# Who starts a tile's sum: ScalarE takes the first expert's weighted bias, with six sum buffers and another order of 20 expert tiles

## The chip, the cores and the metric

The kernel runs on one core of a Trainium2 chip. Its time is device microseconds (us) of one execution; a lower number is better. The core has engines that run side by side and each execute their own queue of instructions strictly in order: TensorE (PE, matrix products and transposes; its weight loads are listed apart as PEld), VectorE (DVE), ScalarE (ACT) and GpSimd (POOL). SyncE (SP) issues DMAs. An instruction that has to wait for another engine, or for a DMA to land, holds up everything that stands behind it in its own queue.

## What is computed

The input `x` is 16 rows of 512 tokens, 128 numbers each, in float32. With `xn` the layer-normalised `x`, the result is

```
x + attention(xn) + experts(xn)
```

Attention is linear with a decay: `scores = (q k^T) * decay^(distance)`, causal, then `scores @ v @ o_w`. The experts are a mixture of four small networks, of which each token uses two:

```
logits = xn @ router_w + router_b + load_balancer
rw, sel = top_k(logits, 2);  rw = softmax(rw)
e0 = (silu(xn @ w1) * (xn @ w3)) @ w2
e1 = gelu(linear chain of xn @ c1w + c1b) @ c2w + c2b
e2 = two layer norms and a relu network on xn, then @ gen_w + gen_b
e3 = gelu(xn @ ml_w1 + ml_b1) @ ml_w2 + ml_b2
out = sum over the two chosen experts of  rw * e
```

So a token's result begins with weight times bias: experts 1, 2 and 3 have an output bias (`c2b`, `gen_b`, `ml_b2`), expert 0 has none.

## The kernel before

**Sorting tokens by pair of experts.** There are six pairs of experts and six lists in DRAM (`LISTS`, L28). Each list is cut into tiles of two to four chunks of 128 tokens; there are 20 tiles and 66 chunks, which is a little room over the 64 chunks of tokens. The 16 rows are taken in five groups (2, 2, 4, 4, 4 rows). When a group is normalised and its router logits are there, VectorE finds each token's pair and its place in the list (`route`, `count`, `placed`), and POOL scatters the normalised rows to the lists with one indirect DMA for each chunk (`send`, 64 of them, L489). A tile may be loaded when the group that fills it has been sent; `TURN` (L38) gives the order of the 20 tiles and each one's group.

**One row.** `load_x` (L218) fetches it on SP; VectorE takes its moments (`stats`, L458 to L462), POOL the inverse square root (`inv`, L467), VectorE the offset (`offs`, L472), ScalarE writes the normalised row into the buffer that is later sent (`norm`, L477), PE transposes it (`turn`), ScalarE copies that out of PSUM (`turned`), PE multiplies by the q, k, v and router weights (`proj`), ScalarE copies q, k, v (`values`) and VectorE the logits (`logits`, L579). Rows x0 to x10 have buffers of their own and are fetched at once in the first microseconds; x11 to x15 wait for buffers.

**Attention** goes in four quads of four rows (`attention`, L762): `keys` (PE) needs the `values` of the quad's last row, then `score` (PE), `scored` (VectorE, four instructions), `near` (PE), `nsum` (VectorE), `outs` (PE), `total` (VectorE) and `store` (SP).

**One tile** (`Tile.steps`, L996), called @k by its place in `TURN`: load `L` (SP), transpose `T` (PE), copy `TT` (ScalarE); `B`, the weighted biases that start the sum `o`; for each of the two experts its hidden products (`ga`, `gb`, `H`, `U`, `F` on PE; the functions on ScalarE; the products on VectorE), its output products `Y` on PE and the joins `J` on VectorE (`o = y * weight + o`, L946); and for each chunk a scatter `X` on POOL that adds `o` to the output in DRAM (66 of them, L489). Expert 2 has two layer norms on the way. Each of them goes PE, VectorE (`Su`, `Sv`), POOL (`Iu`, `Iv`), VectorE (`Ou`, `Ov`), ScalarE (`Nu`, `Nv`), PE (`Zu`, `Zv`).

**The order of the work.** All these steps are handed to a small planner in the kernel (`emit`, L158). It knows a cost in us for each step, a rank, a number of buffers for each kind of tile (`ROOM`, L115) and the times from which inputs are there; for row b among the first eleven it takes 4.75 + 1.25 b us (L804). It simulates the engines, always takes the step that can start first (within 0.25 us the one of lowest rank), and calls its function; the instructions then stand in each engine's queue in that order. `AHEAD` (L46) shifts the ranks of rows, tiles, biases and quads. So a change of a cost, a rank or a buffer count moves instructions in every queue. Where PE would stand idle early on, the planner puts single matmuls of ones, `fill0` to `fill24` (L356), whose results nobody reads.

**The biases in before** (`biases`, L882) are all on VectorE: one `tensor_scalar` for each chunk (L891, 66 in all), and one `scalar_tensor_tensor` more for each chunk of a tile that has no expert 0 (L893, 38 in all). `o` has four buffers.

Of the kernel before, what the change touches and what calls it, by code (L numbers as in the profile page):

```python
# [10 lines left out]
AF = mybir.ActivationFunctionType  # L11
ALU = mybir.AluOpType
# [7 lines left out]
GROUPS = (2, 2, 4, 4, 4)  # L20
# [5 lines left out]


LISTS = [  # L28
    ((0, 1), (3, 4, 4, 4)), ((0, 2), (3, 2)), ((0, 3), (4, 4)),
    ((1, 2), (3, 3, 4, 3)), ((1, 3), (2, 4, 3, 4, 4, 3)), ((2, 3), (3, 2)),  # L30
]
NL = len(LISTS)
LR = 16 * 512
# [2 lines left out]


TURN = [  # L38
    ((1, 2), 0, 1), ((1, 3), 0, 0), ((0, 1), 0, 1), ((0, 2), 0, 3), ((0, 1), 1, 2), ((1, 2), 1, 2),
    ((1, 2), 2, 4), ((1, 2), 3, 4), ((0, 1), 2, 3), ((2, 3), 0, 3), ((1, 3), 1, 2), ((1, 3), 2, 2),  # L40
    ((0, 1), 3, 4), ((2, 3), 1, 4), ((0, 3), 0, 3), ((1, 3), 3, 3), ((0, 2), 1, 4), ((1, 3), 4, 4),
    ((0, 3), 1, 4), ((1, 3), 5, 4),
]
FILL = 25

AHEAD = {"rows": -2.0, "tiles": 62.0, "biases": -5.0, "quads": (9.0, -36.0, -27.0, -27.0)}  # L46
LAST = 3


# [39 lines left out]
def decay_attention__plus__routed_experts(  # L89
# [10 lines left out]
    nc = tc.nc  # L100
    B, T, D = x.shape
    NC = T // P
# [12 lines left out]
    ROOM = {  # L115
        "bank": 8, "pay1": 2, "pay2": 5, "x": 11, "xnT": 3, "qkv": 2, "kT": 1, "qT": 1, "vs": 1, "S": 1, "sc": 4, "far": 1, "rT": 1,
        "xg": 4, "xT": 3, "th": 2, "h0": 1, "h1": 1, "h3": 1, "f": 1, "uv": 2, "z": 2, "h2": 2,
        "h2T": 1, "z2T": 1, "o": 4,
    }

    LATE = {"x": 3.0, "o": 3.2, "pay1": 2.6, "pay2": 2.6}
# [29 lines left out]
    PE, V, A, G, S = "PVAGS"  # L151
# [100 lines left out]
    F, M, C, R = views(fold_sb, FOLD), views(main_sb, MAIN), views(cols_sb, COLS), views(rows_sb, ROWS)  # L252
# [507 lines left out]
    quads = []  # L760

    def attention(b, a):  # L762

        rank = 5.0 * (b + QUAD - 1) + AHEAD["quads"][b // QUAD]
        of = range(QUAD)
# [23 lines left out]
    for g, m in enumerate(GROUPS):  # L789
# [3 lines left out]
        for b in range(first, first + m):  # L793
            k = NC * (b - first)
            r = Row(b, work, lambda c, k=k, q=q: q.entry(k + c)[:, :D])
            lg = q.lg[:, :, k : k + NC]
            rank = 5.0 * b - AHEAD["rows"] - (120.0 if b < 2 else 0.0)
            ends = [f"store{b}"]
# [29 lines left out]
            if b % QUAD == QUAD - 1:  # L828
                attention(q0, quads[-1])
        rank = 5.0 * (first + m) - AHEAD["rows"] - 50.0  # L830
        n = NC * m
# [17 lines left out]
    BIAS = {1: "c2b", 2: "gen_b", 3: "ml_b2"}  # L849

    class Tile:
# [30 lines left out]
        def biases(s):  # L882

            s.o = s.get("o", s.n, D)
            es = [e for e in s.pair if e in BIAS]
            for i, e in enumerate(es):
                w, bias = s.weight(e), R[BIAS[e]]
                for c in range(s.n):
                    o = s.o[:, c, :]
                    if i == 0:  # L890
                        nc.vector.tensor_scalar(o, bias, w(c), None, ALU.mult)  # L891
                    else:
                        nc.vector.scalar_tensor_tensor(o, bias, w(c), o, ALU.mult, ALU.add)  # L893

        def gate(s, i):
            s.ga = {**getattr(s, "ga", {}), i: bank(f"a_ps_{s.name}_{i}")[:, : s.N]}
# [99 lines left out]
        def steps(s, k, g, ranks):  # L996

            s.k, n, u = k, s.n, 0.2155 * s.n
            copy = 0.025 + 0.1125 * n
            biased, both = copy + 0.09, 0.06 + 0.135 * n  # L1000
            name = lambda q: f"{q}@{k}"

            def step(q, eng, us, fn, after=(), takes=(), rank=0.0):
                add(name(q), eng, us, fn, [name(a) if isinstance(a, str) else a for a in after],
                    [(kind, [name(e) for e in ends]) for kind, ends in takes], ranks + rank)
# [3 lines left out]
            parts = [range(c, min(c + size, n)) for c in range(0, n, size)]  # L1009
            joins = [f"J{e}.{c[0]}" for e in s.pair for c in parts]  # L1010
# [5 lines left out]
            def result(e, m, after, rank=0.0):  # L1016

                for i, c in enumerate(parts):
                    step(f"Y{e}.{c[0]}", PE, m * u / n * len(c), lambda c=c: s.y(e, c), ["B", *after] if i == 0 else [f"Y{e}.{parts[i - 1][0]}"],
                         [("bank", [f"J{e}.{c[0]}"])], rank + ending * (2.0 * i - (e == s.pair[1])))  # L1020
                    step(f"J{e}.{c[0]}", V, 0.26 * len(c), lambda c=c: s.joined(e, c), [f"Y{e}.{c[0]}"], rank=-2.0)
            last = sum(GROUPS[: g + 1]) * NC
            step("L", S, 2.3, s.load, [(f"send{g}.{NC * GROUPS[g] - 1}", 0.0)], [("xg", ["T", "to", "B", *joins])], -50.0)
            users = [f"{q}{i}" for e in s.pair for q, m in {0: (("ga", 4), ("gb", 4)), 1: (("H1", 2),), 2: (("U", 1),), 3: (("H3", 4),)}[e] for i in range(m)]
            step("T", PE, n * 0.11, s.turn, [(name("L"), 4.0)], [("bank", ["TT"]), ("xT", users)], -8.0)
            step("TT", A, copy, s.turned, ["T"], rank=-8.0)
            step("to", V, 0.08, s.numbers, [(name("L"), 4.0)])
            step("B", V, n * (0.2 if 0 in s.pair else 0.46), s.biases, [(name("L"), 4.0)], [("o", [f"X{c}" for c in range(n)])], AHEAD["biases"])
            if 0 in s.pair:
                for i in range(4):  # L1030
                    step(f"ga{i}", PE, u, lambda i=i: s.gate(i), ["TT"] + [f"ga{i - 1}"][: i], [("bank", [f"m{i}"]), ("th", [f"h{i}"])] + ([("h0", [f"Y0.{end}"])] if i == 0 else []))
# [11 lines left out]
            if 2 in s.pair:  # L1043
                def normed(key, after, bank, ends, head):
                    step(f"S{key}", V, 0.6 + 0.35 * n, lambda: s.summed(key), after, rank=head)
                    step(f"I{key}", G, 0.4 + 0.2 * n, lambda: s.inv(key), [f"S{key}"], rank=head - 100.0)
                    step(f"O{key}", V, 0.08, lambda: s.offs(key), [f"I{key}"], rank=head - 100.0)
                    step(f"N{key}", A, 0.02 + 0.385 * n, lambda: s.norm(key), [f"O{key}"], [("z", ends)], head)

                step("U0", PE, u, s.syn, ["TT"], [("bank", ["Su"]), ("uv", ["Nu"])], -7.0)  # L1050
                normed("u", ["U0"], "U0", ["R", "Zu"], -7.0)
                step("R", V, 0.12 + 0.27 * n, s.residual, ["Nu"], [("h2", ["Sv"])], -7.0)
                step("Zu", PE, n * 0.11, lambda: s.zturn("u"), ["Nu"], [("bank", ["ZZu"]), ("h2T", ["F0", "F1"])], -6.5)
                step("ZZu", A, copy + 0.2, lambda: s.zturned("u"), ["Zu"], rank=-6.5)
                for i in range(2):
                    step(f"F{i}", PE, u, lambda i=i: s.hid("f", i, M["f1w"], lambda: s.h2T), ["ZZu"] + [f"F{i - 1}"][: i], [("bank", [f"AF{i}"])] + ([("f", ["F"])] if i == 0 else []), -6.0)
                    step(f"AF{i}", A, biased, lambda i=i: s.act("f", i, 2, AF.Relu, C["f1b"]), [f"F{i}"], rank=-6.0)
                step("F", PE, 2 * u, s.ff2, ["AF0", "AF1"], [("bank", ["Sv"]), ("uv", ["Nv"])], -6.0)
                normed("v", ["F", "R"], "F", ["Zv"], -5.5)
                step("Zv", PE, n * 0.11, lambda: s.zturn("v"), ["Nv"], [("bank", ["ZZv"]), ("z2T", [f"Y2.{end}"])], -5.0)  # L1060
                step("ZZv", A, copy + 0.2, lambda: s.zturned("v"), ["Zv"], rank=-5.0)
                result(2, 1, ["ZZv"], -4.0)
# [3 lines left out]
    tiles = {}  # L1066
# [5 lines left out]
    for k, (pair, i, g) in enumerate(TURN):  # L1072
        tiles[pair, i].steps(k, g, AHEAD["tiles"] + 12.0 * k)

# [5 lines left out]
    f = "p g l -> p (g l)"  # L1080
# [29 lines left out]
    with tc.For_i(0, trips, 1) as i:  # L1110
# [20 lines left out]
        s = Dense(0, 3, 0, NC, "row")  # L1131
# [9 lines left out]
        for e in BIAS:  # L1141
            for c in range(NC):
                o = s.o[:, c, :]
# [78 lines left out]
```

## Time and profile before

| what | us |
|---|---|
| median of six runs | 302.32 (301.92 to 302.73) |
| the profiled execution, its own time | 302.81 |
| its span, first to last instruction | 301.1 |
| PE busy | 286.5, 2218 matmul instructions |
| VectorE busy | 203.5, 827 instructions |
| ScalarE busy | 159.8, 347 instructions |
| POOL busy | 204.7, 238 instructions |
| last output product of the last tile ends, last scatter starts | 291.3, 293.7 |

The profiled execution is 1.7 us longer than its span (time around the first and last instruction), and 0.5 us longer than the median of the runs. In the profile a line such as `L489` is the line of the kernel that recorded the instruction; the lines L146 (matmul) and L484 (transpose) are helpers that all PE work goes through. A group's row gives the count, the busy time in us and the mean length of one in ns. An engine's instructions overlap a little, so their distance from start to start is shorter than the length that is listed.

### The profile page before, as it was taken

Reading aid. Unit: us, or ns where it says so; the run is one execution under the profiler, and the core shown is the slowest. Engines: PE = TensorE matmul, PEld = TensorE weight load, DVE = VectorE, ACT = ScalarE, POOL = GpSimd, SP = SyncE. Lnnn points to the kernel's source line nnn. Section 1 sums busy time; section 2 is a strip of 40 time slices with the busy share of each in tenths; the row PEclk is TensorE's granted clock in tenths of the full one; section 3 lists DMA queues with packets and bytes.
Section 4 is the critical chain, followed back from the end, with each engine's and each line's share of the span. In section 5 each row is a group of like instructions: output and inputs, shape, how many; then the busy total and the mean of one; then the engine's idle time right before and its main releaser. Section 6 shows DMA issues by size and latency. Waiting matters only on the chain.

```text
span 301.1 us, 6542 instructions
## 1 busy us (share of the span) xinstructions
PE 286.5 (95%) x2218; PEld 223.2 (74%) x2218; DVE 203.5 (68%) x827; ACT 159.8 (53%) x347; POOL 204.7 (68%) x238
## 2 busy tenths in 40 slices
PE   8999999899999999999999999999999999999970
PEld 7899777788775768766678888758847797765960
DVE  3898899899878397848897676449747146635330
ACT  2889896966971324844473765524443326507020
POOL 5648978778877768888877758886642457183472
PEclk9999999999999999999999999999999999999995
DMA  6994174916321251335533243553222224023032
GB/s 174 307 300 170 42 242 120 312 51 188 102 98 61 89 184 57 69 30 76 69 29 50 25 85 48 73 75 37 36 23 50 49 27 59 7 27 26 8 31 22
DMA packets 33236, 26.55 MB, mean 88 GB/s; under 512 B 3632, under 2 KB 30512, under 8 KB 33072
## 3 DMA queue, kind: packets, MB, share of 16 engines
q0 software_dynamic: 11552, 8.92, 20.0%
q1 hardware_dynamic: 21072, 16.44, 18.2%
q10 hardware_dynamic: 576, 0.74, 0.8%
q8 instruction: 19, 0.31, 0.4%
q14 instruction: 17, 0.14, 0.2%
HBM read 12.09 MB, written 14.12 MB: 87 GB/s over the span
## 4 chain that ended last, share of the span: by engine, by line
PE 74%; DVE 12%; DMA 5%; POOL 3%; issue 2%; ACT 1%; ACTq 0%; POOLq 0%; SPq 0%; DVEq 0%
PE y_ps L146 27%; PE h_ps L146 15%; PE b_ps L146 8%; PE a_ps L146 8%; PE f_ps L146 7%; DVE sc L642 2%; DMA fold_sb<-in_fold_dram 2%; PE xT_ps L484 2%; PE proj_ps L146 2%; PE u_ps L146 2%; DVE st_x L458 1%; DMA x<-in_x_dram 1%; DMA lists<-pay,idx 1%; POOL rstd_x L467 1%; POOL out_dram L489 1%
## 5 line engine op out<-in xcount | busy, mean ns | idle before, releaser
L489 POOL DMA_INDIRECT out_dram<-o,to x66 | 103.7, 1571 | 52.1 <-DVE o L946 38.6
L489 POOL DMA_INDIRECT lists<-pay,idx x64 | 63.7, 995 | 18.6 <-issue 5.6
L946 DVE SCALAR_TENSOR_TENSOR o<-y_ps,xg,o 128x128 f32<-128x128 f32 x132 | 38.3, 344 | 48.6 <-PE y_ps L146 48.2
L146 PEld LDWEIGHTS y_ps<-main_sb,h 128*128 128x128 f32 x456 | 53.9, 192 | 5.4 <-issue 3.8
L146 PE MATMUL y_ps<-main_sb,h 128*128 128x128 f32 x456 | 54.9, 275 | 0.3 <-ACT kT L630 0.3
L922 ACT ACTIVATE h<-h_ps,cols_sb 128x512 f32<-128x512 f32 (+2 forms) x40 | 24.3, 612 | 29.8 <-PE h_ps L146 29.1
L146 PE MATMUL h_ps<-xT,main_sb 128*128 128x512 f32 (+2 forms) x80 | 33.7, 520 | 1.0 <-DVE x L701 1.0
L922 ACT ACTIVATE h<-h_ps,b_e 128x512 f32<-128x512 f32 (+2 forms) x28 | 17.6, 628 | 24.9 <-PE h_ps L146 24.6
L905 ACT ACTIVATE th<-a_ps 128x512 f32<-128x512 f32 (+2 forms) x32 | 17.2, 543 | 23.3 <-PE a_ps L146 23.0
L146 PE MATMUL a_ps<-xT,w_sb 128*128 128x512 f32 (+2 forms) x64 | 29.2, 543 | 0.0
L908 DVE SCALAR_TENSOR_TENSOR th<-th,a_ps 128x512 f32<-128x512 f32 (+2 forms) x32 | 19.4, 616 | 13.3 <-ACT th L905 12.9
L477 ACT ACTIVATE pay<-x,off_x,rstd_x 128x128 f32<-128x128 f32 x64 | 26.3, 486 | 2.9 <-DVE off_x L472 2.3
L146 PEld LDWEIGHTS y_ps<-sw_w2h,h 128*128 128x128 f32 x224 | 26.0, 192 | 1.0 <-issue 0.4
L146 PE MATMUL y_ps<-sw_w2h,h 128*128 128x128 f32 x224 | 26.6, 275 | 0.0
L146 PE MATMUL b_ps<-xT,w_sb 128*128 128x512 f32 (+2 forms) x64 | 26.0, 541 | 0.3 <-ACT xT L873 0.3
L146 PE MATMUL h_ps<-xT,w_e 128*128 128x512 f32 (+2 forms) x56 | 25.1, 539 | 0.0
L467 POOL TENSOR_TENSOR rstd_x<-ve_x,neg_half 128x4 f32<-128x4 f32 x16 | 16.5, 1035 | 8.9 <-DVE ve_x L462 5.9
L146 PEld LDWEIGHTS h_ps<-xT,main_sb 128*128 128x128 f32 x80 | 13.9, 191 | 8.6 <-issue 4.5
L913 DVE TENSOR_TENSOR h<-th,b_ps 128x512 f32<-128x512 f32 (+2 forms) x32 | 19.4, 618 | 1.2
L146 PEld LDWEIGHTS b_ps<-xT,w_sb 128*128 128x128 f32 x64 | 11.7, 190 | 10.0 <-issue 6.5
L146 PEld LDWEIGHTS a_ps<-xT,w_sb 128*128 128x128 f32 x64 | 11.1, 190 | 7.8 <-issue 5.0
L458 DVE BATCH_NORM_STATS2 st_x<-x 128x6 f32<-128x128 f32 x64 | 13.8, 279 | 4.6 <-DMA x<-in_x_dram 4.5
(185 smaller groups left out, 490.7 us busy)
## 6 DMA issues: line engine op xcount, KB each, us to landing
x<-in_x_dram SPq DMA_DIRECT2D x16, 256.0 KB, 5.3
out_dram<-x SPq DMA_DIRECT2D x16, 256.0 KB, 2.8
xg<-lists SPq DMA_DIRECT2D x9, 288.0 KB, 2.9
xg<-lists SPq DMA_DIRECT2D x8, 216.0 KB, 2.5
main_sb<-in_main_dram SPq DMA_DIRECT2D x1, 1216.0 KB, 7.4
out_dram<-o,to POOLq DMA_INDIRECT x66, 3.3
lists<-pay,idx POOLq DMA_INDIRECT x64, 2.3
lists<-none SPq DMA_DIRECT2D x6, 144.0 KB, 5.3
```

Source lines behind the costliest of these rows:

```text
L146: nc.tensor.matmul(o, lhsT, rhs, start=start, stop=stop)
L458: nc.vector.bn_stats(st[:, c, :], v(c))
L467: nc.gpsimd.tensor_tensor(rstd, ve, neg_half[:, :n], ALU.pow)
L477: nc.scalar.activation(o(c), v(c), AF.Identity, bias=off[:, c : c + 1], scale=rstd[:, c : c + 1])
L484: nc.tensor.transpose(pt[:, ts(c, P)], z(c), ident)
L489: i = nc.gpsimd.indirect_dma_start(out=o, out_offset=bass.IndirectOffsetOnAxis(ap=index, axis=0), in_=src, in_offset=None, bounds_check=n ...
L642: nc.vector.tensor_tensor(s.sc[i], s.sbanks[i].rearrange("p (c t) -> p c t", c=NC), near.unsqueeze(1).to_broadcast([P, NC, P]), ALU.mult,)
L905: nc.scalar.activation(s.th[i], s.ga[i], AF.Tanh, scale=0.5)
L908: nc.vector.scalar_tensor_tensor(s.th[i], s.th[i], 1.0, s.ga[i], ALU.add, ALU.mult)
L913: nc.vector.tensor_tensor(s.h0[:, i, :], s.th[i], s.gb[i], ALU.mult)
L922: nc.scalar.activation(getattr(s, key)[:, i, :], s.hb[key, i], func, bias=bias[:, i : i + 1])
L946: nc.vector.scalar_tensor_tensor(o, s.py[e, chunks[0]][:, c, :], w(c), o, ALU.mult, ALU.add)
```

## The change

The first weighted bias of a tile is written by ScalarE, as an activation `Copy` with the weight as its scale (66 instructions); the second, for the 38 chunks of tiles without expert 0, stays on VectorE as a step of its own, `B2`. `o` gets six buffers. Two lists are cut differently (the chunks of each list stay the same in number), the 20 tiles have a new order, the rank shifts in `AHEAD` are new, and some of the planner's costs are set anew. The load buffer `xg` is released by the joins without naming `B`.

```diff
 LISTS = [
-    ((0, 1), (3, 4, 4, 4)), ((0, 2), (3, 2)), ((0, 3), (4, 4)),
-    ((1, 2), (3, 3, 4, 3)), ((1, 3), (2, 4, 3, 4, 4, 3)), ((2, 3), (3, 2)),
+    ((0, 1), (3, 4, 4, 4)), ((0, 2), (2, 3)), ((0, 3), (4, 4)),
+    ((1, 2), (2, 4, 4, 3)), ((1, 3), (2, 4, 4, 3, 4, 3)), ((2, 3), (3, 2)),
 ]
 TURN = [
-    ((1, 2), 0, 1), ((1, 3), 0, 0), ((0, 1), 0, 1), ((0, 2), 0, 3), ((0, 1), 1, 2), ((1, 2), 1, 2),
...
+    ((1, 3), 0, 0), ((0, 2), 0, 2), ((0, 1), 0, 1), ((1, 2), 0, 1), ((1, 2), 1, 2), ((0, 2), 1, 4),
+    ((0, 1), 1, 2), ((2, 3), 0, 3), ((2, 3), 1, 4), ((1, 3), 1, 2), ((1, 3), 2, 3), ((1, 2), 2, 4),
+    ((1, 3), 3, 3), ((1, 2), 3, 4), ((1, 3), 4, 4), ((0, 1), 2, 3), ((0, 3), 0, 3), ((0, 1), 3, 4),
     ((0, 3), 1, 4), ((1, 3), 5, 4),
 ]
-AHEAD = {"rows": -2.0, "tiles": 62.0, "biases": -5.0, "quads": (9.0, -36.0, -27.0, -27.0)}
+AHEAD = {"rows": 10.0, "tiles": 28.0, "biases": 49.0, "quads": (-6.0, -153.0, -174.0, -6.0)}
...
-        "h2T": 1, "z2T": 1, "o": 4,
+        "h2T": 1, "z2T": 1, "o": 6,
...
         def biases(s):
             s.o = s.get("o", s.n, D)
-            es = [e for e in s.pair if e in BIAS]
-            for i, e in enumerate(es):
-                w, bias = s.weight(e), R[BIAS[e]]
-                for c in range(s.n):
-                    o = s.o[:, c, :]
-                    if i == 0:
-                        nc.vector.tensor_scalar(o, bias, w(c), None, ALU.mult)
-                    else:
-                        nc.vector.scalar_tensor_tensor(o, bias, w(c), o, ALU.mult, ALU.add)
+            e, w = s.biased()[0], s.weight(s.biased()[0])
+            for c in range(s.n):
+                nc.scalar.activation(s.o[:, c, :], R[BIAS[e]], AF.Copy, scale=w(c))
...
+        def more_bias(s):
+            e, w = s.biased()[1], s.weight(s.biased()[1])
+            for c in range(s.n):
+                o = s.o[:, c, :]
+                nc.vector.scalar_tensor_tensor(o, R[BIAS[e]], w(c), o, ALU.mult, ALU.add)
...
-            biased, both = copy + 0.09, 0.06 + 0.135 * n
+            biased, both = copy + 0.09, 0.14 + 0.135 * n
...
-                    step(f"J{e}.{c[0]}", V, 0.26 * len(c), lambda c=c: s.joined(e, c), [f"Y{e}.{c[0]}"], rank=-2.0)
+                    step(f"J{e}.{c[0]}", V, 0.06 + 0.265 * len(c), lambda c=c: s.joined(e, c), [f"Y{e}.{c[0]}"], rank=-2.0)
...
-            step("L", S, 2.3, s.load, [(f"send{g}.{NC * GROUPS[g] - 1}", 0.0)], [("xg", ["T", "to", "B", *joins])], -50.0)
+            step("L", S, 2.3, s.load, [(f"send{g}.{NC * GROUPS[g] - 1}", 0.0)], [("xg", ["T", "to", *joins])], -50.0)
...
-            step("B", V, n * (0.2 if 0 in s.pair else 0.46), s.biases, [(name("L"), 4.0)], [("o", [f"X{c}" for c in range(n)])], AHEAD["biases"])
+            step("B", A, 0.05 + 0.385 * n, s.biases, [(name("L"), 4.0)], [("o", [f"X{c}" for c in range(n)])], AHEAD["biases"])
+            if 0 not in s.pair:
+                step("B2", V, 0.05 + 0.275 * n, s.more_bias, ["B"], rank=AHEAD["biases"])
...
-                    step(f"N{key}", A, 0.02 + 0.385 * n, lambda: s.norm(key), [f"O{key}"], [("z", ends)], head)
+                    step(f"N{key}", A, 0.06 + 0.395 * n, lambda: s.norm(key), [f"O{key}"], [("z", ends)], head)
```

What the change does to the queues can be read from the two built programs. The beginning of VectorE's queue stands thus (steps that both have up to `d_s` left out):

```
before: d_s u_w logits0 offs2 stats4 offs3 stats5 logits1 offs4 route0 offs5 count0 stats6 weigh0 logits2 placed0 logits3 offs6 route1 count1 weigh1 stats7 placed1 u_b b_e1 logits4 offs7 stats8 scored0
after:  d_s stats4 logits0 offs2 offs3 stats5 offs4 stats6 logits1 offs5 route0 offs6 count0 u_w logits2 stats7 placed0 logits3 weigh0 route1 logits4 offs7 count1 weigh1 stats8 placed1 scored0
```

PE's queue up to the first quad's keys is `... turn3 place0 proj2 proj3 m2< fill18 fill19 fill20 fill21 fill22 turn4 keys0` in before and `... turn3 proj2 place0 fill18 turn4 proj3 proj4 keys0` in after; ScalarE's is `... norm3 turned2 tanh0 turned3 hold0 wide_bias m1 values2 norm4 values3` in before and `... norm3 turned2 norm4 turned3 tanh0 turned4 values2 values3` in after. POOL's first `send` stands behind `inv6` in before and behind `inv7` in after. SP's queue is the same up to the first list load. In after, `values2` and `values3` wait for the `logits` of their row, which stand first at the same PSUM bank.

## The prediction

> **What bounds the kernel now.** I read the page's busy times and slices first, then the same busy times by stretches of 20 us, then what PE and the others waited for, then the timeline of the first 110 us.
>
> ```profile
> PE 286.5 (95%) x2218; PEld 223.2 (74%) x2218; DVE 203.5 (68%) x827; ACT 159.8 (53%) x347; POOL 204.7 (68%) x238
> PE   8999999899999999999999999999999999999970
> DVE  3898899899878397848897676449747146635330
> ```
>
> PE is the bound: it idles 14.6 of 301.1 us. VectorE is near full only in slices 2 to 13 of 7.5 us each, up to some 97 us. The stretches (first columns: PE, PEld, DVE, ACT, POOL busy) say where PE's idle time lies:
>
> ```profile
> 0.00:20.00 20.00, 18.10 (x131) 16.61 (x131) 13.58 (x96) 12.23 (x35) 10.76 (x42) 1.00 0.84 250
> 20.00:40.00 20.00, 18.86 (x261) 16.95 (x259) 16.98 (x99) 17.28 (x45) 16.09 (x18) 1.00 0.42 148
> 40.00:60.00 20.00, 18.71 (x261) 15.68 (x259) 18.05 (x79) 17.05 (x43) 16.00 (x52) 1.00 0.74 226
> 100.00:120.00 20.00, 20.00 (x139) 14.63 (x138) 15.13 (x45) 7.40 (x14) 15.08 (x17) 1.00 0.35 113
> ```
>
> From 100 to 280 us every stretch has PE at 20.00 of 20. The idle time is 1.9 us in the first 20 us (1.4 of it before the first matmul), 3.6 from 20 to 100 us, and 9 in the tail after the last product at 291.3 (last scatters and shutdown). Busy spans have modelled ends, so I also took from the timeline each start less the start before and less the form's own distance: between 18 and 100 us PE stands still for 6.6 us. That is all that a better order can give back outside the tail.
>
> PE's own work does not change: the chunks of each list stay the same (5 for (0,2), 13 for (1,2), 20 for (1,3)), so do the 25 fills. Its last 23 steps, the products of the last tile and most of the one before it, have the same order, so the tail stays. **So the question is only how long PE stands still.**
>
> **The biases themselves.** By shape:
>
> ```profile
> L891 DVE TENSOR_SCALAR o<-rows_sb,xg 128x128 f32<-128x128 f32 x66 | 15.1, 301 | 0.3 <-DMA out_dram<-o,to 0.3
> L893 DVE SCALAR_TENSOR_TENSOR o<-rows_sb,xg,o 128x128 f32<-128x128 f32 x38 | 10.9, 343 | 0.0
> L651 ACT ACTIVATE vs<-qkv,d_s 128x128 f32<-128x128 f32 x4 | 1.6, 393 | 0.0
> L477 ACT ACTIVATE z<-uv,off_u,rstd_u 128x128 f32<-128x128 f32 x23 | 9.7, 482 | 3.1 <-DVE off_u L472 3.1
> ```
>
> VectorE loses 66 instructions, 0.196 us from start to start in the timeline: 12.9 us. The 38 of L893 stay. ScalarE's new form is not in the trace; the nearest row is L651, the same `Copy` with a scale for each partition on 128 elements (0.292 from start to start), and the upper end is L477, scale and offset (0.385). So ScalarE gains 66 x 0.292 = 19.3 us, at most 25.4; I take 19.3. L651 runs between gelus with no table load listed for it, so no load is added. All of this lies beside PE: after 100 us VectorE has 3 to 11 us to spare in 20 and ScalarE 7 to 12. I cost it at nothing there; without that cover ScalarE's 19.3 us would be the price. Before 55 us only two of the 66 stood on VectorE, so in the start the relief is 0.4 us.
>
> The Trainium skill, "ScalarE: Activation LUTs", section "Rules for kernel authors", says that a plain multiplication belongs on VectorE and not on ScalarE. By the rows (301 against 393 ns) it costs 66 x 0.092 = 6 us of engine time more, which is nothing in the end time as long as PE is the bound; only where ScalarE were the bound would it add those. The skill's "SBUF — State Buffer", section "Who interferes with whom", says that a `tensor_scalar` within SBUF can lock GpSimd out of a port pair. In this trace the 14 output scatters that overlap an L891 took 1.56 us and the 52 others 1.57, so I take no gain for POOL; by the rule it would be up to 66 x 0.28 = 18 us of POOL time.
>
> **The new order: the start.** VectorE now takes `stats4` before `logits0` and `offs2`, and `stats6` before `logits1` and `route0`. Both wait for rows on their way from DRAM.
>
> ```profile
> 13.65 0.87 DVE L458 BATCH_NORM_STATS2 st_x<-x 128x6 f32<-128x128 f32 x4 [0.79 <-DMA x<-in_x_dram]
> rows_sb<-in_rows_dram SPq DMA_DIRECT2D x1, 512.0 KB, 7.3
> ```
>
> The first line is `stats4`: x4 landed at 13.6. The second is the 512 KB load that SP issues at 10.85, just ahead of x6 (11.4). The trace's landing marks of x3 to x8 end at 10.1, 13.6, 14.5, **18.9**, 19.7 and 20.5. The planner counts on x6 at 4.75 + 1.25 x 6 = 12.25. In before this does not show, since `stats6` comes at 19.1. In after:
>
> - `stats4` 13.65 to 14.95 (1.25 to 1.3 for one row), `logits0`, `offs2`, `offs3`, `stats5` to 16.5. Then VectorE stands until x6 is there: `stats6` 18.95 to 20.2.
> - Behind it `logits1`, `offs5`, `route0` (2.3 us, by its rows from 16.46 to 18.72), done at 22.8; in before it began at 16.46. `count0` 23.3, `u_w`, `logits2`, `stats7` 25.0, `placed0` 25.6, `logits3` 25.7.
> - ScalarE's `values3` waits for `logits3`: done at 26.3. PE's `keys0` needs it: 26.4 to 27.3. In before it ended at 24.3.
> - POOL's first `send` stands behind `inv7`, which needs `stats7`: 26.4, against 22.3 before.
>
> **From there I walked the queues by hand**, each engine in its order, with distances from start to start out of the rows (PE 0.109 to 0.112 for 128 columns, 0.43 for 512; `scored` 0.60; `total` 0.60; `norm` 1.54; send 1.28; scatter 1.85; inverse 1.25, for a tile 0.9 to 1.9) and 0.15 to 0.2 us for each hand-over. "Work" is PE's own rows up to there; time less work is what PE has lost.
>
> | PE step, its end | before: time, work, lost | after: walk, work, lost |
> |---|---|---|
> | keys0 | 24.3, 20.8, 3.5 | 27.3, 20.3, 7.0 |
> | near0 | 33.3, 28.1, 5.2 | 35.1, 27.0, 8.1 |
> | near4 | 48.1, 39.3, 8.8 | 48.6, 38.0, 10.6 |
> | keys8 | 58.9, 48.4, 10.5 | 62.2, 49.9, 12.3 |
> | near8 | 67.2, 55.8, 11.4 | 69.2, 56.9, 12.3 |
> | keys12 | 86.5, 74.3, 12.2 | 82.8, 70.2, 12.6 |
> | outs12 | 107.6, 93.2, 14.4 | 110.2, 94.9, 15.3 |
>
> The start loses 3.5 us against before. From near0 to keys12 the new order wins most of it back: there is more tile work between a quad's dependent steps (16.6 us of PE work from the end of `keys12` to that of `score12`, where before had 5.7), and the stalls of before at 35.9 (`outs0`, 0.6), 53.2 (1.0) and 85 to 92 us (four of 0.3 to 0.5) are covered. Lost at 107 us: 0.9 more than before.
>
> **After 107 us**, before loses nothing. In after POOL starts 4 us later and runs without a pause until the sends are out, as it did in before from 22 to 121 us:
>
> ```profile
> L489 POOL DMA_INDIRECT lists<-pay,idx x64 | 63.7, 995 | 18.6 <-issue 5.6 <-DMA lists<-pay,idx 3.7 <-ACT pay L477 3.4
> ```
>
> (Each has 0.3 us behind it that is POOL's own: 64 x 1.28 = 82 us.) Among group 3's and 4's sends now stand the inverses of the norms of tiles @3, @1 and @4, and four scatters before the last six sends. PE's `Zv@4` comes 0.35 us before POOL's late `Iv@4` lets it go, `Zv@7` 0.3 and `Zu@11` 1.0 (POOL is behind with scatters there). Sum 1.65. The waits of the six `o` buffers cost nothing by the walk: the buffer that `B@5` needs is free at 156, and ScalarE comes to it at 157.
>
> **Sum**: +0.9 + 1.65, less 0.3 for taking the bias at 0.292 where the walk had 0.385 = +2.2 us. On the profiled span 301.1 becomes 303.3, its own time 302.81 becomes 305.0, and the median 302.3 becomes **304.5 us**.
>
> **Rivals.**
>
> 1. *The wait for x6 is covered, and the change wins* (301.3; 0.17). The same walk with x6 there in time gives 106.9 for `outs12`, lost 12.0, 2.4 less than before; with the 1.65 after it and the 0.3, the sum is -1.0. It decides at the landing of x6: each us that it comes before 18.9 gives back some 1.4, and it is even at about 17.3. For it: VectorE's work up to the fourth quad's `scored` is the same in both, and later PE has tile work to hide behind. Against: the landing mark, with the same DMAs in the same order in front of it. At its best, all 6.6 us of standing still go and the time is 295.7 (0.05).
> 2. *ScalarE and POOL fall behind* (308; 0.13). `B` has a place in ScalarE's queue: if its `o` buffer is not free, all activations behind it wait. It decides when POOL's scatters run more than 1.5 us later than in the walk (`B@5`: 156 against 157); then each us costs one, at `B@5` and at each `Zu`, `Zv`. Price 2 to 5 us on top.
> 3. *Nothing to be seen* (302.3; 0.12): the loss of the start is won back wholly, as the order after near0 already does in large part.
>
> **Numbers.** My forecast, slower by 1 to 4 us, has 0.53. About 0.2% (0.6 us) is what a measurement of this kernel can tell from no change. Faster by more: 0.17 + 0.05 = 0.22. Within: 0.12. Slower: 0.53 + 0.13 = 0.66. The range goes from 300.7 (the lower part of rival 1 left out) to 307.5 (the upper part of rival 2). Cases of the forecast's sign alone: 303 to 307.
>
> **What would show it.** Right: a wait of VectorE at L458 for the x DMA of about 2.4 us near 16.5 to 19 us; `route0` (L507) beginning near 20.4; the first list scatter at 26; PE busy in 20 to 40 us below 18.9; L891 gone, a ScalarE row of 66 at 0.39 us in its place, 38 left on VectorE; small gaps of PE after 100 us at the z transposes (L484). Wrong: `keys0` done by 24.5, PE's stretches to 100 us fuller than before, or a `B` on ScalarE that waits for the output scatter for more than 1 us.

## The result, and the profile after

The changed kernel takes 304.15 us in the median of 19 runs (302.17 to 308.52), the kernel before 302.29 us in the median of 41 runs (301.82 to 303.76). The change makes the kernel 1.86 us slower by the medians. The ratio is 1.0055, with a 95% interval of 1.0042 to 1.0069, which is 1.7 us: it leaves out the two slowest runs (307.18 and 308.52). The profiled execution of the changed kernel is one of its quicker ones: 303.0 us, span 301.3 us.

What stands out beside the median is the spread: 6 us, where before has 2. Below it turns out to be a part of the answer.

The page of the changed kernel, to be held against the first fence of the prediction (busy times, then the slices of PE and VectorE in tenths):

```profile
PE 286.0 (95%) x2218; PEld 223.5 (74%) x2218; DVE 190.3 (63%) x761; ACT 176.9 (59%) x413; POOL 204.8 (68%) x238
PE   8879999999999999999999999999999999999970
DVE  3868978798898984883536667574346273637330
```

PE's work is the same (2218 matmuls, 286 us). VectorE has lost 13 us and ScalarE gained 17. But PE's third slice (15 to 22.5 us) has gone from 9 to 7. The stretches of the changed kernel (PE, PEld, DVE, ACT, POOL busy, then the granted clock):

```profile
0.00:20.00 20.00, 16.15 (x115) 14.47 (x116) 11.77 (x85) 12.45 (x33) 11.25 (x43) 1.00 0.86 256
20.00:40.00 20.00, 19.07 (x264) 17.40 (x263) 16.93 (x100) 14.41 (x40) 13.60 (x14) 1.00 0.32 118
40.00:60.00 20.00, 18.93 (x241) 16.07 (x241) 17.07 (x75) 19.21 (x49) 16.27 (x54) 1.00 0.72 216
80.00:100.00 20.00, 20.00 (x199) 18.18 (x202) 17.73 (x77) 13.89 (x40) 15.53 (x17) 1.00 0.34 108
100.00:120.00 20.00, 20.00 (x168) 13.47 (x165) 15.18 (x52) 10.44 (x22) 14.88 (x16) 1.00 0.42 124
```

PE has lost 1.95 us in the first 20 us (18.10 before) and gained 0.2 in each of the next two stretches and 1.0 from 80 to 100 us, where the kernel before had 18.98:

```profile
80.00:100.00 20.00, 18.98 (x201) 13.59 (x201) 13.94 (x54) 9.74 (x25) 15.23 (x17) 1.00 0.25 82
```

So the loss is in one place, ahead of 20 us. VectorE's timeline there (start, length, then in brackets the idle time just before and what ended it):

```profile
13.13 0.87 DVE L458 BATCH_NORM_STATS2 st_x<-x 128x6 f32<-128x128 f32 x4 [0.98 <-DMA x<-in_x_dram]
18.07 0.87 DVE L458 BATCH_NORM_STATS2 st_x<-x 128x6 f32<-128x128 f32 x4 [2.05 <-DMA x<-in_x_dram]
19.55 0.35 DVE L507 TENSOR_TENSOR dif<-lg 128x24 f32<-128x24 f32 x3
```

The second line is `stats6`, which waits 2.05 us for x6; the third is the begin of `route0`, 3.1 us later than in the kernel before:

```profile
16.46 0.35 DVE L507 TENSOR_TENSOR dif<-lg 128x24 f32<-128x24 f32 x3
```

What PE waited for, its three longest waits in the changed kernel:

```profile
PE fill_ps L146 <- DVE lg L579: 1.6, 1, 1.6
PE busy_ps L146 <- DVE none L239: 1.4, 1, 1.4
PE sc_ps L146 <- ACT qT L634: 0.8, 2, 0.4
```

The longest wait of PE is that of a fill, a matmul whose result nobody reads. It needs a PSUM bank that `proj1` holds until VectorE has taken `logits1` (L579), and `logits1` stands behind `stats6`.

### The profile page after: what moved, and what is told of

It reads as the page before. It is cut to its first block, busy times and chain, and to the rows that moved or that the text cites. A ratio compares the mean times of both kernels' runs of the same rounds, so it can differ in the third digit from the quotient of the medians.

```text
span 301.3 us, 6558 instructions
## 1 busy us (share of the span) xinstructions
PE 286.0 (95%) x2218; PEld 223.5 (74%) x2218; DVE 190.3 (63%) x761; ACT 176.9 (59%) x413; POOL 204.8 (68%) x238
## 4 chain that ended last, share of the span: by engine, by line
PE 80%; ACT 7%; DMA 5%; DVE 3%; issue 1%; POOLq 1%; SPq 1%; ACTq 0%; POOL 0%
PE y_ps L146 28%; PE h_ps L146 15%; PE b_ps L146 8%; PE a_ps L146 8%; PE f_ps L146 7%; PE proj_ps L146 3%; DMA fold_sb<-in_fold_dram 2%; DMA x<-in_x_dram 2%; PE xT_ps L484 2%; ACT pay L477 2%; PE u_ps L146 2%; ACT h L925 1%; PE xnT_ps L484 1%; PE sc_ps L146 1%; PE nt_ps L146 1%
## 5 line engine op out<-in xcount | busy, mean ns | idle before, releaser
L489 POOL DMA_INDIRECT out_dram<-o,to x66 | 103.0, 1561 | 53.8 <-DVE o L949 36.9
L925 ACT ACTIVATE h<-h_ps,cols_sb 128x512 f32<-128x512 f32 (+2 forms) x40 | 24.1, 612 | 26.1 <-PE h_ps L146 25.6
L146 PE MATMUL h_ps<-xT,main_sb 128*128 128x512 f32 (+2 forms) x80 | 32.8, 518 | 0.0
L146 PE MATMUL b_ps<-xT,w_sb 128*128 128x512 f32 (+2 forms) x64 | 26.1, 541 | 0.0
L925 ACT ACTIVATE h<-h_ps,b_e 128x512 f32<-128x512 f32 (+2 forms) x28 | 17.1, 621 | 14.9 <-PE h_ps L146 14.6
L887 ACT ACTIVATE o<-rows_sb,xg 128x128 f32<-128x128 f32 x66 | 21.3, 394 | 0.4 <-DMA xg<-lists 0.4
```

Source lines behind the costliest of these rows:

```text
L146: nc.tensor.matmul(o, lhsT, rhs, start=start, stop=stop)
L489: i = nc.gpsimd.indirect_dma_start(out=o, out_offset=bass.IndirectOffsetOnAxis(ap=index, axis=0), in_=src, in_offset=None, bounds_check=n ...
L887: nc.scalar.activation(s.o[:, c, :], R[BIAS[e]], AF.Copy, scale=w(c))
L925: nc.scalar.activation(getattr(s, key)[:, i, :], s.hb[key, i], func, bias=bias[:, i : i + 1])
```

## The experiments

Twelve runs. Theory 1 is that of the prediction: VectorE's wait for x6, and what stands behind it, cost the time. Its rival: the start is won back, and the loss is in the rest of the order, on ScalarE or on POOL. Theory 3 came with the spread. Each execution has a mean granted clock, the share of full speed at which TensorE was clocked. In the changed kernel's executions it goes from 0.973 to 0.993, and the long ones are those with a low clock. Theory 3 says that PE's standing still near 18 us makes the clock fall.

| its 21 executions (the median takes 19 of them) by mean granted clock | number | mean time, us |
|---|---|---|
| 0.989 to 0.993 | 13 | 303.4 |
| 0.984, 0.985 | 4 | 304.5 |
| 0.977, 0.978 | 3 | 306.3 |
| 0.973 | 1 | 308.5 |

Several kernels below have the very same order on PE, 2218 matmuls each. So their traces can be laid over each other: how much later does each matmul start than the same one of another kernel? That gives a table at the end of this section.

### 1. `stats6` behind `count0`

Only VectorE's queue changes (`inv6` keeps its place on POOL). The planner's order is collected in `seq` first and issued after the moves.

```diff
+        for n, m, behind in (("stats6", "count0", 1), ("inv6", "stats6", 1), ("offs6", "stats7", 1),):
+            seq.remove(n); seq.insert(seq.index(m) + behind, n)
```

> The changed kernel with one step moved: stats6 stands behind count0 in VectorE's queue instead of ahead of logits1 (offs6 goes behind stats7, the inverse stays where it is on POOL). Nothing else is another. Theory 1 (VectorE's wait for x6 and what is queued behind it cost the time): route0 begins near 16.6 us instead of 19.6, the matmul that stood 1.6 us at 18 us no longer does, and the time is 304.15 less 2.4 to 3.3 us: 301.3 (300.8 to 301.8), faster than before. Rival (the start is won back anyway, and the loss lies in the rest of the order, on ScalarE or on POOL): 303.7 to 304.5. Theory 3 (the wide spread of the changed kernel, 302.2 to 308.5, goes with granted clocks of 0.973 to 0.993 and comes from PE standing still at 18 us): here the spread is no wider than before's 2 us, whatever the median.

Measured: 301.78 us (301.27 to 302.59, 12 runs), ratio to before 0.9979 (0.9965 to 0.9992). VectorE's timeline of this kernel, `route0` and `stats6`:

```profile
17.10 0.34 DVE L507 TENSOR_TENSOR dif<-lg 128x24 f32<-128x24 f32 x3
19.65 0.85 DVE L458 BATCH_NORM_STATS2 st_x<-x 128x6 f32<-128x128 f32 x4
```

Nothing waits for x6 any more, and `route0` comes 2.45 us sooner. PE's row for the same fills shows 14 of them in one piece, where the changed kernel had 8, a hole (a stretch in which PE stands still), and 6:

```profile
16.88 1.73 PE L146 MATMUL fill_ps<-idle 128*128 128x128 f32 x14
```

This move makes the changed kernel 2.4 us faster by the medians and puts it ahead of before. Theory 1 stands, its rival falls. Not all of the wait's price is gone: `keys0` now stands 0.96 us for ScalarE's `values3`, whose `logits3` still has `stats6` ahead of it on VectorE. The spread is 1.3 us and all clocks are 0.988 to 0.994, as theory 3 wants.

### 2. x6 ahead of the constant rows

```diff
-    nc.sync.dma_start(rows_sb[:, tenth:], rows[tenth:].partition_broadcast(P))
     for b in range(6, ROOM["x"]):
         load_x(b)
+    nc.sync.dma_start(rows_sb[:, tenth:], rows[tenth:].partition_broadcast(P))
```

> The changed kernel with the 512 KB load of the constant rows moved on SP from just ahead of x6 to behind x10; every engine's order stays. Theory 1: x6 lands some 1.5 us sooner (512 KB at the 300 to 340 GB/s that the slices of 15 to 25 us show), VectorE's wait shrinks from 2.05 to about 0.5 us, and at 1.4 us of time per us of landing the median is 302.1 (301.3 to 302.9). The constant rows come at about 21 us, and their first reader stands on VectorE at about 28, so that costs nothing. Rival (the start is won back anyway): 303.7 to 304.5. Theory 3: narrower spread in proportion to how much of PE's hole at 18 us goes.

Measured: 301.18 us (300.57 to 302.07, 11 runs), ratio to before 0.9955 (0.9939 to 0.9971). VectorE's timeline of this kernel:

```profile
16.05 0.87 DVE L458 BATCH_NORM_STATS2 st_x<-x 128x6 f32<-128x128 f32 x4
17.52 0.35 DVE L507 TENSOR_TENSOR dif<-lg 128x24 f32<-128x24 f32 x3
```

`stats6` starts 2.02 us sooner and without a wait. The gain is larger than the expected range: I had left it 0.5 us of waiting. Every queue of the engines is that of the changed kernel; the place of one DMA on SP is worth 2.97 us.

### 3. The same two steps moved in the kernel before

`stats4` ahead of `logits0`, `stats6` ahead of `logits1`, as the change has them, and nothing else:

```diff
+        for n, m, behind in (("stats4", "logits0", 0), ("stats6", "logits1", 0),):
+            seq.remove(n); seq.insert(seq.index(m) + behind, n)
```

> The kernel before with two steps of VectorE's queue moved as the change moves them: stats4 ahead of logits0, stats6 ahead of logits1. All else is the kernel before. Theory 1: VectorE waits for x6 as after does, route0 begins near 20 instead of 16.5, and the time is 302.3 + 2.4 to 3.5 = 305.3 (304.7 to 305.8). It has less tile work after 35 us to win that back with than the changed kernel. Rival (the wait is hidden by later slack): 302.3 to 302.8. Theory 3: if PE stands still near 18 us here too, the runs spread over more than 4 us.

Measured: 308.79 us (306.42 to 309.99, 6 runs), ratio 1.0201 (1.0168 to 1.0234). The sign is theory 1's, the size is twice what I expected. VectorE's and PE's lines from the timelines of this kernel:

```profile
18.64 0.87 DVE L458 BATCH_NORM_STATS2 st_x<-x 128x6 f32<-128x128 f32 x4 [2.68 <-DMA x<-in_x_dram]
20.11 0.35 DVE L507 TENSOR_TENSOR dif<-lg 128x24 f32<-128x24 f32 x3
```

```profile
20.64 0.71 PE L146 MATMUL fill_ps<-idle 128*128 128x128 f32 x4 [1.47 <-ACT qkv L576]
```

PE stands here too. Laid over the trace of before, its matmuls start 3.65 us later from 20 us to the end. Two of the six runs have a clock of 0.989 and 0.992 and take 306.4 and 306.7; the other four, at 0.979 to 0.981, take 308.7 to 310.0. So there are two prices: about 4 us for the wait, and 2 to 3.5 more in the runs with a low clock, of which none is traced here. The spread is 3.6 us, a little under the 4 that theory 3 asked for.

### 4. The first bias back on VectorE

```diff
-                nc.scalar.activation(s.o[:, c, :], R[BIAS[e]], AF.Copy, scale=w(c))
+                nc.vector.tensor_scalar(s.o[:, c, :], R[BIAS[e]], w(c), None, ALU.mult)
```

> The changed kernel with its order of steps untouched, but the first expert's weighted bias (66 instructions) on VectorE by the old form, as a product with the weight, at the same places of the program. Theory 1 (the biases lie beside PE's work on either engine): 304.15 within 0.5 us: 303.7 to 304.7. Rival A (ScalarE's 66 activations of 0.39 us hold up PE): faster, 302.5 to 303.6. Rival B (VectorE's relief between 60 and 110 us is worth something: 9 instructions of 0.2 us stand there): slower by up to 2 us, 304.8 to 306.2.

Measured: 305.94 us (304.30 to 308.53, 6 runs), ratio 1.0103 (1.0069 to 1.0136). Slower than the changed kernel, as rival B has it, but three of the six runs have a low clock (0.981 to 0.984), so this run alone could not say how much of it is the biases. It caught something else. Its profiled execution is its slowest, x6 is 1.4 us later than in the changed kernel's, and PE's hole is longer:

```profile
20.92 0.94 PE L146 MATMUL fill_ps<-idle 128*128 128x128 f32 x6 [2.82 <-DVE lg L579]
```

The stretches of this execution by the limits of its clock records (the clock is the third figure from the end):

```profile
18.65:22.07 3.42, 1.15 (x10) 1.15 (x11) 2.52 (x20) 1.69 (x5) 1.01 (x1) 1.00 0.80 249
22.07:25.48 3.41, 3.41 (x19) 3.41 (x17) 2.94 (x21) 0.79 (x2) 0.00 (x0) 0.50 0.90 333
25.48:28.89 3.41, 3.41 (x18) 3.41 (x17) 1.46 (x13) 1.70 (x5) 1.01 (x1) 0.50 0.13 54
28.89:32.30 3.41, 2.99 (x64) 2.75 (x67) 2.63 (x20) 3.33 (x11) 2.53 (x3) 1.00 0.09 34
```

In the first stretch PE is busy 1.15 of 3.42 us, and then it runs two stretches at half the clock: 18 and 19 matmuls where the next has 64. Laid over the kernel of experiment 2, PE is 2.98 us late behind the hole and 6.0 us late at 23 us. Half a clock for 6.83 us cost the other 3.0. This is theory 3 seen at work, in one execution.

The Trainium skill, "TensorE: Matmul & The Clock Gate", section "What's actually happening", says that a monitor halves TensorE's clock after a window of some 3.4 us without activity, and that these windows run freely, whatever the kernel does. The records here agree on the window (all but the last, which the end cuts off, are multiples of 3.413 us). On the condition the measurement differs: 2.82 us of standing, with 1.15 us of work in the same window, was enough.

### 5. The first bias on VectorE, without the wait for x6

Experiments 2 and 4 together: the clean way to ask what the biases cost. Three runs of one kernel; the first two could not be read (see 7).

> The changed kernel with x6 loaded early (load of the constant rows behind x10) and the first bias on VectorE again, at the same places of the program: the run with the biases back, without the wait that blurs it. The prediction's step (the biases cost nothing on either engine): 301.2 within 0.4. Rival B (VectorE's relief counts, as 305.9 against 304.15 says): 302.2 to 303.2, with the loss where the 13 or so biases up to 115 us stand, ahead of a scored, a join or a sum that PE waits for. If the 1.8 us came of chance in x6's landing and the clock, it is 301.2.

> The kernel of the run with x6 early and the first bias back on VectorE once more, because the chip of that run held up every kernel by some 38 us (the kernel before took 340.3 there). Expectation as there: 301.2 within 0.4 if the biases cost nothing on either engine; 302.2 to 303.2 if VectorE's relief counts.

> The kernel of the two runs with x6 early and the first bias back on VectorE a third time, since both ran on chips that held up the kernel before as well by 38 us. Expectation as there: 301.2 within 0.4 if the biases cost nothing on either engine; 302.2 to 303.2 if VectorE's relief counts. To be compared with the same kernel with the bias on ScalarE, 301.18 at 302.34 for the kernel before.

Measured in the third: 302.30 us (301.66 to 302.97, 12 runs), ratio to before 0.9997 (0.9985 to 1.0009), clocks 0.988 to 0.994. The same kernel with the bias on ScalarE has 0.9955 (0.9939 to 0.9971). So in this order moving the bias is worth 1.1 us by the medians (1.3 by the ratios, within about 0.6), and the step "I cost it at nothing" was wrong. Where it sits: laid over the other kernel, PE goes from 0.46 us early at 80 us to 0.59 us late at 104 us. It loses 0.2 at a `y` (84 us), 0.1 around 90, 0.25 at a z transpose (92) and, the most, 0.47 at `near12` (102). VectorE's lines ahead of `near12` and the 32 matmuls of `near12` themselves, with the bias on VectorE:

```profile
94.18 0.87 DVE L887 TENSOR_SCALAR o<-rows_sb,xg 128x128 f32<-128x128 f32 x4
99.93 1.28 DVE L642 TENSOR_TENSOR sc<-sc_ps,near 128x512 f32<-128x512 f32 x2
102.04 1.56 PE L146 MATMUL nt_ps<-sc,qkv 128*32 128x128 f32 x32
```

and without it:

```profile
99.13 1.27 DVE L642 TENSOR_TENSOR sc<-sc_ps,near 128x512 f32<-128x512 f32 x2
101.93 1.08 PE L146 MATMUL nt_ps<-sc,qkv 128*32 128x128 f32 x32
```

`scored12` is 0.8 us later with the biases on VectorE, although that execution was 0.46 us ahead at 80 us. Ten of them stand on VectorE there: two at 82.7 us, four at 85.6 and these four at 94.2, at 0.2 us each. From 92 us to `scored12` VectorE has one idle piece of 0.49 us without them, and none with them.

### 6. x4, x5 and x6 ahead of the list fills as well

```diff
+    for b in range(4, 7):
+        load_x(b)
     for l, (_, sizes) in enumerate(LISTS):
...
-    for b in range(4, 6):
-        load_x(b)
-    nc.sync.dma_start(rows_sb[:, tenth:], rows[tenth:].partition_broadcast(P))
-    for b in range(6, ROOM["x"]):
+    for b in range(7, ROOM["x"]):
         load_x(b)
+    nc.sync.dma_start(rows_sb[:, tenth:], rows[tenth:].partition_broadcast(P))
```

> The changed kernel with another order of loads on SP and nothing else: x4, x5 and x6 right behind x3, then the six initial fills of the lists (144 KB each), then x7 to x10, then the 512 KB of constant rows. Theory 1 (VectorE's waits for x rows in the first 20 us set the time): the waits for x4 (1.0 to 1.5 us) and for x6 both go, and the time falls below the 301.2 of the run with the constant rows moved alone: 300.0 (299.3 to 300.8), faster than both kernels. Rival (after x6's wait VectorE has no other that counts; PE's next limit is ScalarE's norms): 301.2 within 0.4. Against both: the list fills land later, and if the first list scatter on POOL, near 23 us, waits for them, it is slower than 301.2.

> The kernel of the run with x4, x5 and x6 ahead of the list fills again, because the chip of that run held up the kernel before as well, by 39 us. Its trace there, up to 26 us where the hold-ups begin, has PE's place0 1.25 us earlier than with x6 early alone. Theory 1: PE never wins back nor loses such a lead later (the wait of the changed kernel, +2.0 us at place0, stood at +1.8 at the end), so the time is 301.2 - 1.2 = 300.0 (299.4 to 300.6). Rival (the lead is used up by the next limit in the first 60 us): 301.2 within 0.4.

Measured in the second run: 300.51 us (300.13 to 301.16, 6 runs), ratio to before 0.9932 (0.9913 to 0.9951): the fastest kernel of this study, 1.8 us faster than before. VectorE's five rows of moments now follow each other by its own work (x2 to x6):

```profile
9.61 0.87 DVE L458 BATCH_NORM_STATS2 st_x<-x 128x6 f32<-128x128 f32 x4 [0.26 <-DMA x<-in_x_dram]
10.99 0.86 DVE L458 BATCH_NORM_STATS2 st_x<-x 128x6 f32<-128x128 f32 x4
12.63 0.86 DVE L458 BATCH_NORM_STATS2 st_x<-x 128x6 f32<-128x128 f32 x4
14.11 0.87 DVE L458 BATCH_NORM_STATS2 st_x<-x 128x6 f32<-128x128 f32 x4
15.44 0.87 DVE L458 BATCH_NORM_STATS2 st_x<-x 128x6 f32<-128x128 f32 x4
```

The gain over experiment 2 is 0.67 us, not the expected 1.2: in this execution place0 is 0.6 us earlier, not 1.25. It still lies in theory 1's range, just below the rival's. What lead there is stays to the end (0.58 us at place0, 0.5 at the last matmul).

### 7. Six runs on chips that held the kernel up

The first runs of 5 and 6, the second of 5 and the three below fell on two chips where the kernel before too took 340 to 342 us. In their profiles PE stands again and again within the attention's products for the first 140 us (one `score` of the old order takes 3.6 us longer than in the trace of before), and the clocks are 0.92 to 0.95; why is not known. The ratios there are 1.0227 (1.0169 to 1.0286), 0.998 (0.9924 to 1.0036) and 1.010 (1.0038 to 1.0162) for the three below in their order, and 1.0195 to 1.0212 for the other three. These times stand for those chips only.

PE busy through VectorE's wait, by three fills that go behind `proj2`, to another bank, with two matmuls more each:

```diff
+            more = name in ("fill15", "fill16", "fill17")
+            pt = ps.tile([P, 512], F32, tag="bank4", name=f"{name}_ps") if more else bank(f"{name}_ps")
-            for _ in range(n):
+            for _ in range(n + 2 * more):
```

> The changed kernel with VectorE's order untouched, so that it waits for x6 as before. On PE the three fills of which the first needs the bank that logits1 gives back go behind the products of the third row's projections (proj2), write to a bank that only PE uses there, and have two matmuls more each: PE has 1.9 us of matmuls to do while place0 waits for VectorE. Theory 3 (PE's standing still near 18 us, where x6 comes late, makes the clock gate halve the clock for one, two or three stretches of 3.41 us, each worth up to 1.7 us of matmuls): granted clock 0.988 to 0.994 in all runs, spread of the times below 2.5 us, median 302.8 to 303.4, which is where the changed kernel's runs with a clock of 0.989 and more lie (302.2 to 304.8). Theory 1 alone (only the wait counts, the clock is chance): 304.15, spread of 5 us, clocks down to 0.975.

The kernel before with the edit of experiment 2 (the control for it):

> The kernel before with the 512 KB load of the constant rows moved on SP to behind x10, as in the changed kernel's run above: the control of that run. Theory 1: before waits for no x row from x6 on (stats6 begins 0.2 us after x6 is there), so nothing is won: 302.3 (302.0 to 302.6), and the 2.97 us that this edit gave the changed kernel belongs to the new order's wait. Rival (the earlier rows are a gain by themselves, for any order): 301.0 to 301.8.

The kernel before with the first bias on ScalarE:

```diff
-                        nc.vector.tensor_scalar(o, bias, w(c), None, ALU.mult)
+                        nc.scalar.activation(o, bias, AF.Copy, scale=w(c))
```

> The kernel before with the first bias on ScalarE (a Copy with a scale for each partition) at the same places of the program; four buffers for the sums, old order. The prediction's step (biases lie beside PE's work): 302.3 within 0.3. Rival B (VectorE's relief counts): 301.0 to 302.0. Rival A (a bias that waits for its buffer holds up all activations behind it on ScalarE): slower, 302.8 to 305, with a row of 66 on ScalarE that waits for the output scatter.

The traces of the last two still show something, because the hold-ups end before 146 us. Laid over the trace of before, PE with an early x6 is 38.2 us late from there to the last matmul: nothing more is lost. With the first bias on ScalarE it falls another 2.5 us behind, in four places: 0.84 at an `f`, 0.46 and 0.45 at two z transposes, 0.69 at a `y`. Each time biases stand on ScalarE just ahead of an activation whose result PE needs. The first of the four, ScalarE and then PE:

```profile
203.40 1.26 ACT L891 ACTIVATE o<-rows_sb,xg 128x128 f32<-128x128 f32 x4
204.57 0.56 ACT L922 ACTIVATE f<-f_ps,cols_sb 128x384 f32<-128x384 f32 x1
```

```profile
205.19 1.05 PE L146 MATMUL f_ps<-main_sb,f 128*128 128x128 f32 x7 [0.58 <-ACT f L922]
```

So at the old order's places the bias on ScalarE does hold up PE, in this one execution; the order has to be made for it.

Open are therefore: whether a warm PE alone would narrow the spread, whether the old order would gain some tenths from an earlier x6 (the wait itself is not in its trace; with an early x6 it is 0.5 us ahead at 24 us, where the hold-ups begin soon after), and what the bias on ScalarE makes of the old order's time on a usual chip.

### All on one scale

How much later PE starts the same matmul than the kernel of experiment 2 does, in us, worked out from the start times in the traces (one execution each):

| kernel | a `fill` ahead of the hole, 17.2 us | `place0`, 20.3 | 30 | 80 | 104 | last matmul, 290.2 |
|---|---|---|---|---|---|---|
| changed | -0.1 | +2.04 | +2.04 | +2.02 | +2.02 | +1.76 |
| 1: `stats6` late | -0.17 | -0.37 | +0.71 | +0.70 | +0.70 | +0.45 |
| 4: bias on VectorE | 0.0 | +3.90 | +5.77 | +5.74 | +6.81 | +7.29 |
| 5: the same, x6 early | -0.42 | -0.43 | -0.43 | -0.46 | +0.59 | +0.33 |
| 6: x4 to x6 first | -0.38 | -0.58 | -0.60 | -0.55 | -0.55 | -0.50 |

Each row reads from left to right: a number that changes is a place where time went or came back, one that stays is a delay that nothing gives back. The changed kernel's 2 us come between 17 and 20 us and stand unchanged at 104 us. 0.26 of them come back at 144 us, at a z transpose; there experiment 2 waits for a late inverse of POOL's and the changed kernel, being later, does not. Experiments 1 and 5 get the same back there, so by these traces the bias is worth 0.8 us at the end (from 0.43 early to 0.33 late).

By medians the change splits up like this. New order with the x rows in time, biases on VectorE: 302.30, nothing won or lost against before's 302.3 (before itself was not measured with an early x6 on a usual chip). First bias on ScalarE: -1.1 (301.18). The wait for x6: +3.0 (304.15), of which 2.0 are its plain length in the trace. The rest I put down to later landings and the clock, without a trace of such a run of the changed kernel itself: its executions at a clock of 0.989 and more have a mean of 303.4, all runs a median of 304.15.

## Why the prediction was right, and where not

The forecast was 304.5 and slower; the time is 304.15. Step by step:

**PE bounds, and only its standing still counts.** Right: 286.0 us of work after, 286.5 before, and every difference above is a hole or a slow clock of PE.

**The biases themselves.** The size was right: 0.393 us by the nearest row, 0.394 measured, and 0.292 from start to start in both. These are the groups of the changed kernel (busy us and mean ns after the bar):

```profile
L489 POOL DMA_INDIRECT out_dram<-o,to x66 | 103.0, 1561 | 53.8 <-DVE o L949 36.9 <-issue 15.6 <-DVE ve_u L462 0.3
L489 POOL DMA_INDIRECT lists<-pay,idx x64 | 63.8, 996 | 18.2 <-issue 9.2 <-ACT pay L477 2.2 <-ACT o L887 0.9
L887 ACT ACTIVATE o<-rows_sb,xg 128x128 f32<-128x128 f32 x66 | 21.3, 394 | 0.4 <-DMA xg<-lists 0.4
L896 DVE SCALAR_TENSOR_TENSOR o<-rows_sb,xg,o 128x128 f32<-128x128 f32 x38 | 11.0, 346 | 0.0
```

The value was wrong. "I cost it at nothing" held for ScalarE in this order: the waits of PE for ScalarE (`sc_ps` 0.8, `far_ps` 0.4) are the same in experiment 5, with the biases on VectorE. In the old order it did not hold (section 7). And the relief of VectorE is a gain of 1.1 us. I looked at VectorE before 55 and after 100 us, and counted its spare time by stretches of 20 us. Between 84 and 103 us it has next to none ahead of `scored12` (experiment 5). My walk had the relief in its queues; only its separate price was missing, and so I could not say that without it the new order wins nothing.

The Trainium skill's rule that a plain multiplication belongs on VectorE ("ScalarE: Activation LUTs", "Rules for kernel authors") agrees with the rows, 321 ns on VectorE (experiment 5) against 394. For the time of this kernel, in its new order, the measurement decides the other way: 1.1 us in favour of ScalarE. The lock of a port pair that a `tensor_scalar` can take by the skill ("SBUF — State Buffer", "Who interferes with whom") does not show in the scatters: an output scatter takes 1561 ns with the biases on ScalarE, and 1556 in experiment 5, with them on VectorE. The 12 there that overlap a bias took 1550 ns, the 54 others 1557. Its groups:

```profile
L489 POOL DMA_INDIRECT out_dram<-o,to x66 | 102.7, 1556 | 54.5 <-DVE o L949 37.0 <-issue 16.0 <-DVE th L911 0.3
L887 DVE TENSOR_SCALAR o<-rows_sb,xg 128x128 f32<-128x128 f32 x66 | 16.0, 321 | 0.5 <-DMA out_dram<-o,to 0.4
```

**The start.** Right in place and kind, and it is the whole loss. VectorE's wait was 2.05 us (2.4 forecast), `route0` began at 19.55 (20.4), the first send at 25.6 (26.4), `keys0` ended at 26.1 (27.3). All are early by the same reason: I took before's landing mark of x6, 18.92, as fixed. It is not: `stats6` found x6 at 18.07 here, 18.64 in experiment 3 and 19.42 in experiment 4, with the same loads ahead of it. I also missed how the wait reaches PE first: not by `proj` or `place0`, but by a fill, whose result nobody reads and which needs a bank behind the same wait. One sign that I had named for being right did not come: PE's 20 to 40 us are at 19.07, not below 18.9, since the whole loss lies ahead of 20 us.

**From near0 to keys12 the order wins most of it back.** As arithmetic against before this held: the walk had 12.0 us lost at `outs12` with x6 in time, at 106.9 us; experiment 2 reaches it at 106.9. Read as "a delay is won back" it is wrong: laid over the kernel without the wait, nothing is won back up to 104 us, and 0.26 of 2.02 us after that.

**After 107 us, 1.65 us.** Too much. The trace has PE gaps of 0.25 us (121.6), 0.28 (182.0) and 0.30 (199.0), together 0.8. There PE waits for ScalarE's `h` (L925), `z2T` (L989) and `xT` (L873), and not for POOL's late inverses as forecast; experiment 5 has the same three, so the biases on ScalarE are not their cause. The list scatters kept pace, and the six `o` buffers cost nothing, as predicted: `L887` waits 0.4 us in all, for loads.

**The rivals.** The first, x6 covered, was given 301.3; made so, the kernel takes 301.18. Its slope of 1.4 us per us of landing is 1.0 in one execution (2.02 us for 2.04) and 1.5 by medians (2.97 us), the clock included. The second, ScalarE and POOL falling behind, did not happen. That the sum came so close is in part luck. For the profiled execution it gave 305.0 us of own time, 2.2 more than before's, and that took 303.0, 0.2 more: the wait for x6 was put 1.3 us too high (3.3 between the two walks, 2.0 between the two traces) and the steps after 107 us 0.8. The median run is 1.15 us above that execution, which I put down to later landings and the slow clock; the sum had neither.

## What to carry to other kernels

Where a planner orders the queues by assumed arrival times, hold them against the landing marks of several traces: here 12.25 us stood in the code for a row that came between 18 and 19.4, and one step ahead of its data cost 3 us, while the place of one DMA brought them back. Lay the traces of two kernels with the same order on the bounding engine over each other, instruction by instruction; a delay at the start then shows at once whether anything gives it back. Price an instruction that changes engines at its place in both queues, not by spare time in stretches of 20 us: here the relief was worth 1.1 us where VectorE's queue was full, and in the old order the same instructions cost PE 2.5 us of one execution where they stood ahead of activations that PE needed.

## What was not expected of the hardware

A hole of 2.82 us in PE's work halved its clock for two stretches of 3.41 us and so cost as much again (3.0 us). Holes of 1.56 and 1.47 us in other profiled executions did not; there PE was busy 1.85 and 1.94 us of the record's stretch of 3.41 us that held the hole, against 1.15. That does not give a limit: on the chips of section 7 half the clock also followed on stretches in which PE was busy for 1.66 to 1.81 us (the run with the old order and an early x6) and up to 2.82 us (the first run of experiment 5). With the wait for x6, 15 of 33 executions (8 of 21, 4 of 6, 3 of 6) had a mean clock of 0.985 or less; without it, in experiments 1, 2, 5 and 6 on the usual chips, none of 41.

Identical loads do not land at identical times: x6 varied by 1.4 us between executions at the same place of SP's queue. An order that just touches a landing time has therefore not one time but a spread of them.
